# FP4 rounding in layer 2: two or three of its last steps on GpSimd, the others on VectorE

## The chip, the cores and the metric

The kernel runs on one core of a Trainium2 chip. A core has TensorE (PE, matrix products and transposes, results in PSUM), VectorE (DVE), ScalarE (ACT), GpSimd (POOL[...]) and SyncE (SP, a queue for DMAs). Each engine works through its own queue in order, and the queues wait for one another by semaphores. The metric is the device time of one execution in microseconds (us); lower is better. The median of three runs before the change is 2027.1 us (2026.68 to 2034.26).

## The reference

Four layers act on x of shape (4, 512, 256) in float32, that is 2048 rows. Each layer adds a cross-attention to a short context and then a feed-forward network. Layers 0, 1 and 3 have routed experts in the feed-forward; layer 2 has a plain one whose inputs and weights are rounded to FP4 in blocks of 16. Only this part is touched:

```python
def fp4_quant_dequant(x):
    xb = x.reshape(shape[:-1] + (shape[-1] // BLOCK, BLOCK))       # BLOCK = 16
    scale = jnp.max(jnp.abs(xb), axis=-1, keepdims=True) / 6.0
    scale = jnp.maximum(scale, jnp.float32(1e-12))
    xn = xb / scale
    idx = jnp.searchsorted(_MID, jnp.abs(xn))
    q = _GRID[idx] * jnp.sign(xn) * scale      # grid 0, 0.5, 1, 1.5, 2, 3, 4, 6
    return q.reshape(shape)

def fp4_linear(x, w):
    return jnp.einsum('bsk,nk->bsn', fp4_quant_dequant(x), fp4_quant_dequant(w))

def _L2_ffn_ref(x, w_gate, w_up, w_down):      # 256 -> 704 -> 256
    gate = fp4_linear(x, w_gate)
    y = fp4_linear(x, w_up)
    h = jax.nn.silu(gate) * y
    return fp4_linear(h, w_down)

x = x + _L2_xattn_ref(_layernorm(x, axis=-1), ctx_1024)
x = x + _L2_ffn_ref(_layernorm(x, axis=-1), L2_ffn_w_gate, L2_ffn_w_up, L2_ffn_w_down)
```

Layer 2's attention picks, for each row, the context row with the largest cosine and adds it ("alignment" below).

## The kernel before

The 2048 rows are held in SBUF as 16 tiles x[t] of 128 rows and 256 columns; four tiles make a group (one batch entry). The kernel runs the layers one after another. Layer 2 is the function `l2`, from about 1375 to 1600 us of the profiled execution.

The rounding is `fp4` (from L1437). `fp4_scale` first makes the block maxima (L1430), the scales (L1433) and their reciprocals (L1434). Then, on VectorE: multiply by the reciprocal into f_y (L1450), mask out the exponent into f_c (L1455), bound it from below and multiply by a constant so that f_c is the number to add (L1456), add f_c (L1457) and subtract it again (L1458), which rounds to the FP4 grid. The last step, multiplying by the scale into the output (L1459), goes to the engine in the argument `last`, and all three callers pass GpSimd. The callers are:

- `l2_weights`, for 18 pieces of the weights, run during layer 0 (278 to 563 us);
- `quantized(t)` in `l2`, for the 256 normalized columns of tile t, giving xq. TensorE transposes xq (L1538, into ps_xq) and ScalarE copies the result to SBUF (xqT, L1540);
- `gated` in `l2`, for the 704 gated columns, giving hq. TensorE transposes hq (L1512, ps_hT), ScalarE copies (hqT, L1513).

The loop over 16 tiles runs `up` (16 matrix-product records into four PSUM banks, ps_f, L1549), then `quantized` of the next tile, then `gated` (ScalarE's SiLU L1559 and VectorE's product h, L1560, two halves), then `down` of the tile before (ps_fd, L1571, and the addition to x, L1572). Among the tiles of one group, the alignment of the next group (`l2_xattn`: L317 to L325, L357, L1405, L691 to L703, L1413 to L1422) and its second normalization (`normed`) are woven in. The buffers f_y, f_c, xq and hq have two copies of each width.

No order is written by hand in this stage: `in_order` covers the routed experts' blocks and some other parts, not `l2`. The framework's planner puts the instructions in each engine's queue, so the order seen in the trace isn't the order of the text; it starts instructions of layer 3 (on GpSimd, the additions of a bias to x, L608) from 1549 us on. On GpSimd the last additions of layer 1's expert results (L1033) end at about 1403 us.

Of the kernel before, what the change touches and what calls it, by code (L numbers as in the profile page):

```python
# [17 lines left out]
ALU = mybir.AluOpType  # L18
# [1017 lines left out]
class Layers(Net):  # L1036
# [397 lines left out]
        nc.vector.reciprocal(rs, sc)  # L1434
        return sc, rs

    def fp4(self, tmp, out, src, last, scale=None):  # L1437


        nc = self.nc  # L1440
        rows, n = src.shape
        G = n // 16

        def blocks(t):
            return t.rearrange("p (g k) -> p g k", k=16)

        sc, rs = scale or self.fp4_scale(src)
        y, c = (tmp(t, n)[:rows] for t in ("f_y", "f_c"))

        nc.vector.scalar_tensor_tensor(  # L1450
            blocks(y), blocks(src), 1.0 - 2.0**-23, rs[:, :, None].to_broadcast([rows, G, 16]), ALU.mult, ALU.mult
        )


        nc.vector.tensor_scalar(c.bitcast(I32), y.bitcast(I32), 0x7F800000, None, ALU.bitwise_and)  # L1455
        nc.vector.tensor_scalar(c, c, 1.0, 1.5 * 2.0**22, ALU.max, ALU.mult)  # L1456
        nc.vector.tensor_tensor(y, y, c, ALU.add)  # L1457
        nc.vector.tensor_tensor(y, y, c, ALU.subtract)  # L1458
        last.tensor_tensor(blocks(out), blocks(y), sc[:, :, None].to_broadcast([rows, G, 16]), ALU.mult)  # L1459

    def l2_weights(self, pool):

        nc, d = self.nc, self.d
        F = 704
        pieces = [(n, at, t * P, 0) for n, at in (("w_gate", W2_GATE), ("w_up", W2_UP)) for t in range(6)]
        pieces += [("w_down", W2_DOWN, t * P, c) for t in range(NC) for c in range(0, F, E)]
        ws = []

        def load():
            name, _, r0, c0 = pieces[len(ws)]  # L1470
            w = pool.tile([P, E], F32, tag="w2in", name="w2in", bufs=3)
            w = w[: min(P, d[name].shape[0] - r0), : min(E, d[name].shape[1] - c0)]
            nc.scalar.dma_start(w, d[name][r0 : r0 + w.shape[0], c0 : c0 + w.shape[1]])
            ws.append(w)

        load()
        load()
        yield
        def turned(k, wq):
            name, at, r0, c0 = pieces[k]  # L1480
            rows, cols = wq.shape
            ps = self.tr.tile([P, NC, P], F32, tag="tr", name="ps_wq")
            wT = pool.tile([P, NC, P], F32, tag="w2T", name="wqT")
            for k, r in enumerate(min(P, cols - f) for f in range(0, cols, P)):
                nc.tensor.transpose(ps[:r, k, :rows], wq[:, k * P : k * P + r], self.ident[:rows, :rows])
                nc.scalar.copy(wT[:r, k, :rows], ps[:r, k, :rows])
                to = at + (c0 // P + k) * E + r0 if name == "w_down" else at + k * F + r0
                nc.scalar.dma_start(self.w2q[:r, to : to + rows], wT[:r, k, :rows])

        wq = None  # L1490
        for k in range(len(pieces)):
            if k:
                turned(k - 1, wq)
            if len(ws) < len(pieces):
                load()
            w = ws[k]
            rows, cols = w.shape
            scale = self.fp4_scale(w)
            yield
            room = pool.tile([P, 3, E], F32, tag="w2y", name="w2y")  # L1500
            y, c, wq = (room[:rows, k, :cols] for k in range(3))
            self.fp4(lambda tag, n: {"f_y": y, "f_c": c}[tag], wq, w, nc.gpsimd, scale)
            yield
        turned(k, wq)

# [9 lines left out]
    def l2(self, moe):  # L1515
        nc = self.nc
        F, H = 704, 352
        with self.room("l2") as pool:
            wq = pool.tile([P, W2_END], F32, tag="w2", name="w2", bufs=1)
            whole = W2_END - E  # L1520
            nc.sync.dma_start(wq[:, :whole], self.w2q[:, :whole])
            nc.sync.dma_start(wq[: F - 5 * P, whole:], self.w2q[: F - 5 * P, whole:])
            wg, wu = (wq[:, a : a + NC * F].rearrange("p (c f) -> p c f", c=NC) for a in (W2_GATE, W2_UP))
            wd = wq[:, W2_DOWN:].rearrange("p (f e) -> p f e", e=E)
            cnT = self.l2_context(pool)
            xns = {}

            def tmp(tag, n):
                return pool.tile([P, n], F32, tag=f"{tag}{n}", name=tag)

            def quantized(t):

                g, i = divmod(t, GT)
                xq = pool.tile([P, E], F32, tag="xq", name="xq")
                self.fp4(tmp, xq, xns[g][:, i], nc.gpsimd)
                ps = self.tr.tile([P, NC, P], F32, tag="tr", name="ps_xq")
                for c in range(NC):
                    nc.tensor.transpose(ps[:, c], xq[:, c * P : (c + 1) * P], self.ident)  # L1538
                xT = pool.tile([P, NC, P], F32, tag="xqT", name="xqT")
                nc.scalar.copy(xT, ps)  # L1540
                return xT

            def up(xT):
                pss = []
                for k in range(2):
                    for w in (wg, wu):
                        ps = self.mm.tile([P, 512], F32, tag="mm", name="ps_f")
                        for c in range(NC):
                            nc.tensor.matmul(  # L1549
                                ps[:, :H], xT[:, c], w[:, c, k * H : (k + 1) * H], start=(c == 0), stop=(c == NC - 1)  # L1550
                            )
                        pss.append(ps)
                return pss

            def gated(pss):
                h = pool.tile([P, F], F32, tag="h", name="h")
                for k in range(2):
                    s = pool.tile([P, H], F32, tag="fs", name="fs")
                    nc.scalar.activation(s, pss[2 * k][:, :H], AF.Silu)  # L1559
                    nc.vector.tensor_tensor(h[:, k * H : (k + 1) * H], s, pss[2 * k + 1][:, :H], ALU.mult)  # L1560
                hq = pool.tile([P, F], F32, tag="hq", name="hq")
                self.fp4(tmp, hq, h, nc.gpsimd)
                return hq

            def down(t, hq):
                hT = pool.tile([P, 6, P], F32, tag="hqT", name="hqT")
                self.rows_to_columns(hq, lambda f0, n, r: hT[:r, f0 : f0 + n])
                po = self.acc.tile([P, 512], F32, tag="acc", name="ps_fd")
                for f in range(6):
                    r = min(P, F - f * P)  # L1570
                    nc.tensor.matmul(po[:, :E], hT[:r, f], wd[:r, f], start=(f == 0), stop=(f == 5))  # L1571
                nc.vector.tensor_tensor(self.x[t], po[:, :E], self.x[t], ALU.add)  # L1572

            def normed(g):
                xns[g] = pool.tile([P, GT, E], F32, tag="l2xn", name="l2xn")
                self.layernorm(g, xns[g])

            for t in range(NT):  # L1580
                moe.load(pool, t, nc.scalar if t // GT == 1 else nc.sync)
            for t in range(2 * GT):
                moe.take(t, nc.vector if t < GT else nc.gpsimd)
            self.l2_xattn(pool, 0, cnT)
            normed(0)
            xT, last = quantized(0), None
            for t in range(NT):
                g, i = divmod(t, GT)
                if g + 1 < B:
                    if i == 0:  # L1590
                        if g + 2 < B:
                            for k in range(GT):
                                moe.take((g + 2) * GT + k, nc.gpsimd)
                        self.l2_xattn(pool, g + 1, cnT)
                    elif i == 2:
                        normed(g + 1)
                pss = up(xT)
                if t + 1 < NT:
                    xT = quantized(t + 1)
                hq = gated(pss)  # L1600
                if t:
                    down(t - 1, last)
                last = hq
            down(NT - 1, last)
# [77 lines left out]
```

## Time and profile before

| What | Value |
|---|---|
| median of three runs | 2027.1 us |
| profiled execution, its own time | 2033.3 us |
| its span, first to last instruction | 2031.5 us |
| mean granted TensorE clock | 0.921 |
| L1457 and L1458 in `l2`, 128x256, undisturbed | about 0.42 us each |
| L1459 to xq, median of 16 | 0.621 us |
| L1459 to hq, median of 16 | 1.386 us |
| L1033, the same 128x256 addition: VectorE, GpSimd (median) | 0.416 us, 0.724 us |
| waits of TensorE's weight loads at L1512 for hq, 1400 to 1600 us | 8.7 us, 10 times |

A group line of the profile gives source line, engine, operation, output from inputs and shapes, the count, then the busy time in us and the mean of one in ns, then the engine's idle time before the group and what ended it. A timeline line gives the start in us, the duration in us, the engine and the instruction; brackets hold idle time before it. A windows line gives for each engine the busy us in that stretch and the number of instructions, then the granted clock. In the 40 slices each digit is the busy share in tenths.

### The profile page before, as it was taken

What the parts mean: (1) busy time and instruction counts of PE and PEld (TensorE: products, weight loads), DVE (VectorE), ACT (ScalarE), POOL (GpSimd) and SP (SyncE); (2) the same over time, 40 slices, a digit from 0 to 9 for tenths busy, and PEclk for the clock granted to TensorE, in tenths of its full rate; (3) what the DMA queues carried; (4) which work ended last, traced back from release to release, by engine and by line L of the source; (5) the groups of instructions that cost most, each with busy time, mean ns of one, the idle gap of its engine ahead of it and who ended that gap; (6) DMA issues with size and microseconds to landing.
All of it is one profiled execution on the core that took longest, in us unless ns stands there. A gap on an engine that the chain in (4) does not pass through costs nothing.

```text
span 2031.5 us, 25639 instructions
## 1 busy us (share of the span) xinstructions
PE 1716.2 (84%) x8740; PEld 975.9 (48%) x8740; DVE 974.0 (48%) x2778; ACT 668.2 (33%) x1254; POOL 420.3 (21%) x590
## 2 busy tenths in 40 slices
PE   4874999999959978899999878994998887599994
PEld 2443666666624533344443344443665443355662
DVE  3644344444445333445454435446899564333333
ACT  3341322222243341335344522223445333122221
POOL 1033011111150010222222322224113112311112
PEclk8986999999979987999999989996899898699997
DMA  9613878787420000000000018772000001598895
GB/s 290 182 43 127 343 292 285 283 292 279 157 93 1 17 23 0 1 1 17 6 3 20 19 34 283 263 270 88 1 0 1 12 4 40 181 313 296 305 316 170
DMA packets 111042, 271.85 MB, mean 134 GB/s; under 512 B 15488, under 2 KB 73024, under 8 KB 100800
## 3 DMA queue, kind: packets, MB, share of 16 engines
q1 hardware_dynamic: 81728, 227.35, 33.0%
q0 software_dynamic: 10176, 28.00, 3.6%
q10 hardware_dynamic: 19008, 14.86, 2.3%
q8 instruction: 70, 1.15, 0.2%
q14 instruction: 60, 0.49, 0.1%
HBM read 220.75 MB, written 49.42 MB: 133 GB/s over the span
## 4 chain that ended last, share of the span: by engine, by line
PE 63%; DVE 14%; ACT 5%; issue 3%; POOL 3%; DMA 2%; SPq 0%; ACTq 0%; DVEq 0%; POOLq 0%
PE ps_gu L938 20%; PE ps_de L980 9%; PE ps_ms L1127 4%; PE ps_mo L1165 3%; DVE mq L1132 2%; PE ps_he L967 2%; PE ps_p L592 2%; PE ps_mx L1142 2%; PE ps_f L1549 2%; POOL xs L827 2%; PE ps_bc L571 1%; PE ps_ms L1130 1%; PE ps_xT L357 1%; PE ps_xe L924 1%; PE ps_cy L577 1%
## 5 line engine op out<-in xcount | busy, mean ns | idle before, releaser
L938 PE MATMUL ps_gu<-e_wgu,e_xT 128*128 128x352 f32 (+1 forms) x1088 | 417.8, 524 | 4.7 <-DVE e_xT L930 0.8
L938 PEld LDWEIGHTS ps_gu<-e_wgu,e_xT 128*128 128x128 f32 x1088 | 197.2, 191 | 143.9 <-issue 74.0
L980 PE MATMUL ps_de<-e_wd,e_hT 128*128 128x256 f32 x932 | 232.3, 385 | 3.8 <-ACT e_hT L288 1.5
L955 DVE TENSOR_TENSOR e_h<-e_s,ps_gu 128x352 f32<-128x352 f32 (+2 forms) x155 | 83.5, 538 | 295.5 <-PE ps_gu L938 226.9
L983 POOL DMA_INDIRECT ys<-e_y,e_to x116 | 112.4, 969 | 522.4 <-ACT e_y L982 399.5
L980 PEld LDWEIGHTS ps_de<-e_wd,e_hT 128*128 128x128 f32 x932 | 172.1, 189 | 79.5 <-issue 42.3
L954 ACT ACTIVATE e_s<-ps_gu 128x352 f32<-128x352 f32 (+2 forms) x155 | 74.0, 477 | 327.6 <-PE ps_gu L938 323.5
L1132 DVE TENSOR_REDUCE mq<-ps_ms 128x2 f32<-128x256 f32 (+3 forms) x128 | 105.7, 825 | 137.8 <-PE ps_ms L1130 136.5
L982 ACT ACTIVATE e_y<-ps_de,e_wt 128x256 f32<-128x256 f32 x116 | 54.9, 473 | 259.4 <-PE ps_de L980 248.1
L1144 ACT ACTIVATE mpr<-ps_mx 128x1024 f32<-128x1024 f32 (+3 forms) x128 | 90.0, 703 | 138.7 <-PE ps_mx L1142 135.5
L1127 PE MATMUL ps_ms<-mkT,mqT 32*128 32x512 f32 (+3 forms) x512 | 111.1, 512 | 22.7 <-DVE mq L1132 21.6
L827 POOL DMA_INDIRECT xs<-xn,e_at x96 | 93.9, 978 | 135.3 <-DVE ln_rs L322 75.7
L1142 PE MATMUL ps_mx<-mqm,mkT 32*128 32x128 f32 (+3 forms) x512 | 105.6, 489 | 1.1 <-ACT mpr L1144 1.1
L1146 POOL TENSOR_SCALAR_AFFINE_SELECT mpr<-mpr 128x256 f32<-128x256 f32 x128 | 51.8, 407 | 238.6 <-ACT mpr L1144 238.5
L1165 PE MATMUL ps_mo<-mpr,va 128*32 128x128 f32 (+3 forms) x512 | 96.4, 457 | 3.0 <-POOL mpr L1146 3.0
L357 PE MATMUL ps_xT<-consts_sb,xn 128*128 128x128 f32 x256 | 52.4, 340 | 50.9 <-ACT xn L325 36.1
L967 PE MATMUL ps_he<-consts_sb,e_h 128*128 128x128 f32 x466 | 76.2, 278 | 11.9 <-DVE e_h L955 7.9
L1549 PE MATMUL ps_f<-w,xqT 128*128 128x352 f32 x256 | 84.7, 472 | 1.2 <-ACT xqT L1540 1.2
L924 PE MATMUL ps_xe<-consts_sb,e_x 128*128 128x128 f32 x232 | 51.4, 292 | 36.6 <-DMA e_x<-xs 33.6
L927 DVE COPY e_xT<-ps_xe 128x256 f32<-128x256 f32 x78 | 33.0, 423 | 98.4 <-PE ps_xe L924 98.4
L537 PE MATMUL ps_cx<-q,kbd 32*128 32x512 f32 x256 | 45.0, 803 | 39.5 <-ACT cpr L543 39.5
L1127 PEld LDWEIGHTS ps_ms<-mkT,mqT 32*128 32x128 f32 x512 | 40.8, 195 | 77.6 <-DVE mq L1132 54.4
(314 smaller groups left out, 2769.0 us busy)
## 6 DMA issues: line engine op xcount, KB each, us to landing
e_wgu<-in_e0gu SPq DMA_DIRECT2D x39, 1408.0 KB, 6.1
e_wgu<-in_e3gu SPq DMA_DIRECT2D x39, 1024.0 KB, 5.4
e_wd<-in_e0d SPq DMA_DIRECT2D x39, 768.0 KB, 5.6
e_wd<-in_e3d SPq DMA_DIRECT2D x39, 512.0 KB, 5.6
e_wgu<-in_e1gu SPq DMA_DIRECT2D x38, 512.0 KB, 4.0
xs<-z SPq DMA_DIRECT2D x16, 1040.0 KB, 15.4
e_x<-xs SPq DMA_DIRECT2D x116, 130.0 KB, 4.9
e_wd<-in_e1d SPq DMA_DIRECT2D x38, 256.0 KB, 4.1
```

Source lines behind the costliest of these rows:

```text
L827: r = nc.gpsimd.indirect_dma_start(out=net.xs, out_offset=bass.IndirectOffsetOnAxis(ap=at[:, k, i : i + 1], axis=0), in_=rows[:, i], in_of ...
L938: nc.tensor.matmul(ps[:, :n], xT[:, c], wgu[:, c, cols], start=(c == 0), stop=(c == NC - 1))
L955: nc.vector.tensor_tensor(h[:, k * H : (k + 1) * H], s, u, ALU.mult)
L967: self.nc.tensor.transpose(ps[:r, f - f0], h[:, f * P : f * P + r], net.ident)
L980: nc.tensor.matmul(po[:, :E], hT[:r, f], wd[:r, f], start=(f == 0), stop=(f == self.nf - 1))
L983: r = nc.gpsimd.indirect_dma_start(out=net.ys, out_offset=bass.IndirectOffsetOnAxis(ap=at, axis=0), in_=y, in_offset=None)
L1127: nc.tensor.matmul(ps[:, r, :n], st.qT[o][rows, diag], st.kT[o][rows, :n], start=True, stop=False)
L1132: nc.vector.tensor_reduce(st.q[:, i, at : at + 2, HD], ps[:, :, :n], AX.X, ALU.max, negate=True)
L1142: nc.tensor.matmul(ps[:, r, :n], st.kT[o][rows, keys], st.qm[o][rows, j * P :], start=True, stop=True)
L1144: nc.scalar.activation(pr[:, :, :n], ps[:, :, :n], AF.Exp, scale=HD**-0.5)
L1165: nc.tensor.matmul(st.po[32 * n : 32 * n + 32, j * P :], st.va[:, j, at : at + 32], pr[:, r, : S - j * P], start=(j == 0), stop=(j == GT - 1),
L1549: nc.tensor.matmul(ps[:, :H], xT[:, c], w[:, c, k * H : (k + 1) * H], start=(c == 0), stop=(c == NC - 1))
```

## The change

`fp4` gets a number, `late`, in place of the engine: so many of the last three steps (add, subtract, multiply by the scale) go to GpSimd, the others stay on VectorE. The list in the new line ends in three GpSimd engines for 3, in VectorE, GpSimd, GpSimd for 2, and in VectorE, VectorE, GpSimd for 1. The weights pass 1, the normalized rows 3, the gated rows 2. What is computed is the same.

```diff
-    def fp4(self, tmp, out, src, last, scale=None):
+    def fp4(self, tmp, out, src, late, scale=None):
...
         nc.vector.tensor_scalar(c, c, 1.0, 1.5 * 2.0**22, ALU.max, ALU.mult)
-        nc.vector.tensor_tensor(y, y, c, ALU.add)
-        nc.vector.tensor_tensor(y, y, c, ALU.subtract)
+        add, subtract, last = ([nc.vector] * 3 + [nc.gpsimd] * late)[-3:]
+        add.tensor_tensor(y, y, c, ALU.add)
+        subtract.tensor_tensor(y, y, c, ALU.subtract)
         last.tensor_tensor(blocks(out), blocks(y), sc[:, :, None].to_broadcast([rows, G, 16]), ALU.mult)
...
-            self.fp4(lambda tag, n: {"f_y": y, "f_c": c}[tag], wq, w, nc.gpsimd, scale)
+            self.fp4(lambda tag, n: {"f_y": y, "f_c": c}[tag], wq, w, 1, scale)
...
-                self.fp4(tmp, xq, xns[g][:, i], nc.gpsimd)
+                self.fp4(tmp, xq, xns[g][:, i], 3)
...
-                self.fp4(tmp, hq, h, nc.gpsimd)
+                self.fp4(tmp, hq, h, 2)
```

## The prediction

> **What bounds the kernel now.** I read the page first for where the change acts, then windows over that stretch, then its groups by form, the chain of waits and the timeline.
>
> ```profile
> span 2031.5 us, 25639 instructions
> PE 1716.2 (84%) x8740; PEld 975.9 (48%) x8740; DVE 974.0 (48%) x2778; ACT 668.2 (33%) x1254; POOL 420.3 (21%) x590
> ...
> PE   4874999999959978899999878994998887599994
> ...
> DVE  3644344444445333445454435446899564333333
> ```
>
> Over the whole span VectorE is busy only 48%, but each slice is 50.8 us, and slices 29 to 31 (1422 to 1574 us) show 8, 9, 9: this is layer 2's feed-forward, the only place where the edited arguments change anything. Windows there:
>
> ```profile
> core 0: us, PE busy (x) PEld busy (x) DVE busy (x) ACT busy (x) POOL busy (x), PEclk, DMA share, GB/s
> 1400.00:1600.00 200.00, 175.06 (x712) 116.52 (x711) 173.15 (x448) 94.64 (x203) 48.05 (x53) 0.93 0.00 1
> ...
> 1485.00:1495.00 10.00, 10.00 (x41) 6.50 (x40) 10.00 (x25) 8.19 (x21) 2.11 (x3) 1.00 0.00 0
> 1545.00:1555.00 10.00, 8.65 (x37) 5.64 (x36) 10.00 (x22) 4.38 (x10) 5.77 (x6) 1.00 0.00 0
> 1555.00:1565.00 10.00, 7.78 (x34) 5.04 (x33) 9.90 (x22) 4.98 (x10) 5.83 (x6) 1.00 0.00 1
> 1565.00:1575.00 10.00, 9.92 (x41) 6.61 (x40) 7.21 (x16) 4.15 (x9) 1.38 (x1) 1.00 0.01 2
> ```
>
> TensorE and VectorE are both nearly full: two limits that take turns. At 1545 to 1565 VectorE is full and TensorE is not; at 1565 it is the other way round. Adding the 10 us windows from 1405 on, TensorE stands idle for 21 us, 5 of them in the first window (filling); so 16 us is all that can be won by removing waits. The chain of waits agrees: of the 179 us in its longest pieces between 1400 and 1600, 91 us lie on TensorE, 77 (0.43) on VectorE, 7 on GpSimd. GpSimd enters six times: as hq at 1429.50, 1494.90, 1565.47, 1575.85, as xq at 1409.16 and 1536.10.
>
> ```profile
> L1457 DVE TENSOR_TENSOR f_y<-f_y,f_c 128x704 f32<-128x704 f32 x16 | 14.1, 881 | 0.1
> L1458 DVE TENSOR_TENSOR f_y<-f_y,f_c 128x704 f32<-128x704 f32 x16 | 14.1, 880 | 0.0
> L1457 DVE TENSOR_TENSOR f_y<-f_y,f_c 128x256 f32<-128x256 f32 x16 | 10.2, 640 | 0.0
> L1458 DVE TENSOR_TENSOR f_y<-f_y,f_c 128x256 f32<-128x256 f32 x16 | 7.3, 456 | 0.0
> L1459 POOL TENSOR_TENSOR hq<-f_y,f_sc 128x704 f32<-128x704 f32 x16 | 22.4, 1400 | 100.5 <-DVE f_y L1458 66.4 <-PE ps_f L1549 11.8 <-PE ps_xq L1538 9.0
> L1459 POOL TENSOR_TENSOR xq<-f_y,f_sc 128x256 f32<-128x256 f32 x16 | 11.6, 726 | 46.2 <-DVE f_y L1458 25.4 <-PE ps_xq L1538 7.5 <-DVE ln_sh L323 5.6
> ```
>
> Rows two to five are the moved operations, except L1457 at 704 columns, which stays. The 256-column add averages 640 ns, though the same form is 420 when nothing disturbs it. The timeline shows why:
>
> ```profile
> 1545.14 0.16 DVE L1433 TENSOR_SCALAR f_sc<-f_am 128x16 f32<-128x16 f32 x1
> 1545.16 1.39 POOL L1459 TENSOR_TENSOR hq<-f_y,f_sc 128x704 f32<-128x704 f32 x1 [2.76 <-DVE f_y L1458]
> 1545.22 0.16 DVE L322 RECIPROCAL ln_rs<-ln_sd 128x4 f32<-128x4 f32 x1
> 1545.31 1.52 DVE L1457 TENSOR_TENSOR f_y<-f_y,f_c 128x256 f32<-128x256 f32 x1
> 1546.60 0.76 PE L1512 MATMUL ps_hT<-consts_sb,hq 128*128 128x128 f32 x5 [1.34 <-POOL hq L1459]
> 1546.75 0.51 DVE L1560 TENSOR_TENSOR h<-fs,ps_f 128x352 f32<-128x352 f32 x1
> ```
>
> The add starts at 1545.31 but ends at 1546.83, 0.28 us after GpSimd's operation ends: it stood still until then, and h, behind it in VectorE's queue, came late.
>
> **What the Trainium skill says.** "SBUF — State Buffer", section "Who interferes with whom": a VectorE instruction with two SBUF inputs, or in a two-port mode, and a GpSimd instruction that reads SBUF exclude one another; whoever starts first keeps the port pair for the whole instruction. The trace agrees, with 1.52 us in place of 0.42, and for the smallest operation too: a 128x16 L1433 at 1495.14 takes 1.27 us beside hq. "Perfetto Trace Analysis", section "Optimizing Scalar/DVE Operations", warns that offloading between these two may therefore not help. "GPSIMD Engine Reference", section "4.1 Engine selection", gives about twice the time for two-input operations; here the same 128x256 addition (L1033, both engines) takes 416 ns on VectorE and 724 on GpSimd, 1.74 times.
>
> **The change part by part.**
>
> The weights' call keeps two steps on VectorE and one on GpSimd: no cost.
>
> Removed from VectorE. Instructions overlap at their ends, so I count start to start: 0.34 us at 256 columns, 0.80 at 704. Per tile 0.34 + 0.34 + 0.80 = 1.48, times 16 = 23.7 us. With the moved adds go their own blocked times: (640 - 420) x 16 = 3.5 and (456 - 420) x 16 = 0.6. Together 27.8 us.
>
> Added to GpSimd. Add and subtract at 256: 0.72 each from L1033, 1.44 x 16 = 23.0. The subtract at 704 is not in the trace; L1459 at 704, whose second input is a repeated scale, takes 1.39 (lower bound), L1033 stretched in proportion gives 0.72 x 704/256 = 1.98 (upper). I take 1.6, x 16 = 25.6. Sum 48.6 us; GpSimd goes from 48 to 97 busy in the 200, so it doesn't become the bound by load.
>
> What it blocks. In 1400 to 1600 VectorE's blocked time, mean less undisturbed mean times count, is 12.4 us: L1457 3.5, L1458 0.6, L1455 1.5, L1433 1.5, L323 1.6, L1450 1.7, L1456 1.1, L1400 0.9. Over 48 us of GpSimd this is 0.26 us per us. The added 48.6 then block 12.6 us. Unknown: the share may be 0 or, if VectorE always meets a port operation next, near 1. At 0.57 (27.8/48.6) VectorE wins nothing. I take 0.26, and VectorE is relieved by 27.8 - 12.6 = 15.2 us, 0.95 per tile. It counts where VectorE is on the path: 0.43 x 15.2 = 6.5 us.
>
> Longer latency. Row to xq: 1.44 in place of 0.68, +0.76. Gated row to hq: 1.6 in place of 0.80, +0.8. On the chain that is four hq and two xq: 3.2 + 1.5 = 4.7 us. Elsewhere the xq lateness is hidden: xq is one or two tiles ahead (done at 1542.39, transposed at 1544.87, cover 2.5 us). Where hq's lateness is hidden, TensorE's matmuls of the next tile (L1549) do it; there is little: TensorE's weight loads wait for hq ten times already.
>
> Waits and queues. The adds now queue on GpSimd behind layer 3's bias additions (L608, 12 times, 10.3 us, from 1549 on); behind a waiting add stands the other row's hq. f_c comes free after GpSimd's subtract, up to about 2 us later; two buffers of each width mean that only the row after next needs it, some 10 us on: nothing, save at the start, where three rows run close together and a 128x16 scale already waits 0.36 us for xq.
>
> Sum against the profiled execution (2033.3 us, span 2031.5): -6.5 + 4.7 = -1.8, so 2031.5. The median of the runs is 2027.1, 6 us below that execution; the same difference gives 2025.
>
> A check by hand with the order kept, port held by whoever asks first. Tile from 1527.06: the subtract runs 1532.57 to 1534.17, two scales and a reciprocal slip between, VectorE reaches the operation of 1537.16 about 0.7 us early; TensorE waits for xqT there until 1536.88 anyway. Tile from 1537.16: add, subtract and scale of xq alternate with L1450, L1455 and L1456, hq's subtract runs 1544.49 to 1546.09, hq ends at 1547.68 (1546.55 before), and the scale behind it holds h back from 1546.75 to 1547.85: 1.1 late. One better, one worse: no clear sign.
>
> **The rivals.** About 0.5% (10 us) is what a measurement of this kernel can tell from no change.
>
> First, VectorE was the real limit, and TensorE closes up: the whole 15.2 counts less one longer first row and last gated row (0.76 + 0.8), -13.6: about 2013. For it: three 10 us windows with VectorE at 9.9 or more and TensorE at 8.7 or less. Against: only 16 us of TensorE idleness exist, part of it behind ScalarE's table loads and layer 2's alignment chain.
>
> Second, slower by one mechanism: GpSimd's back-to-back operations hold the port, a small VectorE operation stands behind them, h and hq come late, and TensorE waits at hq's transposes (L1512). Price: 1.1 us as in the second replay, at the ten tiles where it waits for hq already, 11, and 0.76 + 0.8 at start and end: +12.6, 2040. It decides when the blocked share passes 0.57.
>
> Third, no order is written by hand in this stage, so the planner may arrange the longer GpSimd steps otherwise; this may tip the sum either way by what the replays differ, within the two above.
>
> **How the numbers follow.** No measurable change around 2025: 0.40 (own range 2017 to 2037); faster near 2013: 0.36; slower near 2040: 0.24. With share 0 the sum would be 0.43 x 27.8 - 4.7 = 7 us won; with share 1, 0.43 x 20.8 + 4.7 = 14 lost. The range for 8 in 10 reaches past these to the two rivals: 2007 to 2042.
>
> **What would show it.** Right: VectorE's busy time in this stage falls by some 10 to 16 us while L1433, L1455 and L1450 lengthen; GpSimd's doubles; a GpSimd 256-column addition takes 0.72, the 704-column subtract 1.4 to 2.0; waits of L1512 for hq grow. Wrong: blocked time far off 0.26 per us, an operation of GpSimd outside its bounds, the chain of waits moving wholly to TensorE (first rival) or to GpSimd's f_y and hq (second), or a change outside 1400 to 1600.

## The result and the profile after

The changed kernel is slower: a median of 2045.13 us (2037.37 to 2053.4, 11 runs) against 2033.42 us of the kernel before on the same chip (2026.68 to 2048.35, 11 runs), a ratio of 1.0049 with a 95% interval of 1.003 to 1.0069, that is 6 to 14 us. A second set on another occasion gave 1.0048 (1.0033 to 1.0062). The forecast of 2025 started from 2027.1, the median of three runs; with eleven runs the kernel before stands at 2033.42, so 6.3 of the 20 us between 2025 and 2045.13 were there before the change. The granted TensorE clock does not explain the rest: in the second set it averaged 0.9157, against 0.9145 for the kernel before. The profiled execution took 2040.63 us (span 2038.9), 7.3 more than that of the kernel before. In the changed kernel the line numbers from L1458 on are one higher: L1458 adds, L1459 subtracts, L1460 multiplies, L1513 transposes hq, L1561 makes h.

The loss lies in layer 2. These lines give the first and last start of two operations, L1422 (an alignment is added to x) and the addition of `down` to x, before and after:

```profile
L1422 DVE TENSOR_TENSOR x<-ps_al,x x16: 414/415/425, 1399.4 to 1516.3; 128x256 f32<-128x256 f32 x16
L1572 DVE TENSOR_TENSOR x<-ps_fd,x x16: 410/421/426, 1436.5 to 1598.9; 128x256 f32<-128x256 f32 x16
...
L1422 DVE TENSOR_TENSOR x<-ps_al,x x16: 412/415/426, 1395.3 to 1514.5; 128x256 f32<-128x256 f32 x16
L1573 DVE TENSOR_TENSOR x<-ps_fd,x x16: 411/420/425, 1433.5 to 1602.5; 128x256 f32<-128x256 f32 x16
```

From the first of these to the last the stage takes 199.5 us before and 207.2 after (210.0 in the changed kernel's second profile). The code ahead of it is the same, yet its end moves between 1395 and 1410 us from one execution to the next, so a fixed window of time does not always hold the same work.

The windows view of the changed kernel, with the same stretch of 200 us first and then the 10 us about tile 10; below it the page's line for the whole program:

```profile
core 0: us, PE busy (x) PEld busy (x) DVE busy (x) ACT busy (x) POOL busy (x), PEclk, DMA share, GB/s
1400.00:1600.00 200.00, 166.11 (x693) 112.08 (x694) 159.47 (x384) 92.95 (x199) 93.30 (x91) 0.93 0.00 1
1540.00:1550.00 10.00, 1.96 (x8) 1.04 (x6) 9.83 (x15) 1.69 (x5) 9.86 (x11) 0.78 0.00 0
...
PE 1713.1 (84%) x8740; PEld 977.0 (48%) x8740; DVE 964.2 (47%) x2730; ACT 668.7 (33%) x1254; POOL 471.6 (23%) x638
```

In the 200 us VectorE's busy time fell by 13.7 us (173.15 to 159.47) and GpSimd's rose by 45.3 (48.05 to 93.30). But TensorE's fell too, by 9 us: it does the same work, so less of the work lies in these 200 us. Over the whole program, where nothing else was changed, VectorE's busy time fell by only 9.8 us (974.0 to 964.2; to 965.4 in the second profile) and GpSimd's rose by 51.3 (420.3 to 471.6). In 1540 to 1550 TensorE does almost nothing, while VectorE and GpSimd are full.

The groups by form in the same stretch, of the steps that moved and of their neighbours on VectorE:

```profile
L1459 POOL TENSOR_TENSOR f_y<-f_y,f_c 128x704 f32<-128x704 f32 x16 | 26.9, 1678 | 70.6 <-DVE f_y L1458 68.4 <-DVE l_m L1400 2.2
L1460 POOL TENSOR_TENSOR hq<-f_y,f_sc 128x704 f32<-128x704 f32 x16 | 22.8, 1427 | 1.0
L1459 POOL TENSOR_TENSOR f_y<-f_y,f_c 128x256 f32<-128x256 f32 x16 | 13.0, 811 | 1.0
L1458 POOL TENSOR_TENSOR f_y<-f_y,f_c 128x256 f32<-128x256 f32 x16 | 12.4, 774 | 8.8 <-DVE f_c L1456 8.6 <-DVE f_sc L1433 0.2
L1450 DVE SCALAR_TENSOR_TENSOR f_y<-l2xn,f_rs 128x256 f32<-128x256 f32 x16 | 10.6, 661 | 0.1
...
L1455 DVE TENSOR_SCALAR f_c<-f_y 128x256 int32<-128x256 int32 x16 | 8.7, 546 | 0.1
```

The added GpSimd time is 26.9 + 13.0 + 12.4 = 52.3 us. The steps of the normalized rows that stayed on VectorE took over the blocking of the steps that left: L1450 at 256 columns now averages 661 ns (477 before), L1455 546 (275 before).

The waits view, TensorE's weight loads, first before and then after; the three numbers are the sum in us, the count and the longest:

```profile
PEld ps_hT L1512 <- POOL hq L1459: 8.7, 10, 2.2
...
PEld ps_sim L1405 <- DVE xnT L290: 1.1, 1, 1.1
...
PEld ps_hT L1513 <- POOL hq L1460: 22.2, 10, 10.3
...
PEld ps_sim L1405 <- DVE xnT L290: 6.8, 3, 4.5
```

The timeline of seven of the ten waits for hq, brackets holding the wait; the last two lines are tiles 10 and 11 of the kernel before:

```profile
1428.62 0.53 PEld L1513 LDWEIGHTS ps_hT<-consts_sb,hq 128*128 128x128 f32 x5 [2.19 <-POOL hq L1460]
...
1436.17 0.53 PEld L1513 LDWEIGHTS ps_hT<-consts_sb,hq 128*128 128x128 f32 x5 [1.34 <-POOL hq L1460]
...
1487.30 0.53 PEld L1513 LDWEIGHTS ps_hT<-consts_sb,hq 128*128 128x128 f32 x5 [1.42 <-POOL hq L1460]
...
1498.39 0.53 PEld L1513 LDWEIGHTS ps_hT<-consts_sb,hq 128*128 128x128 f32 x5 [2.35 <-POOL hq L1460]
...
1532.98 0.42 PEld L1513 LDWEIGHTS ps_hT<-consts_sb,hq 128*128 128x128 f32 x4 [1.42 <-POOL hq L1460]
...
1551.98 0.93 PEld L1513 LDWEIGHTS ps_hT<-consts_sb,hq 128*128 128x128 f32 x5 [10.25 <-POOL hq L1460]
...
1597.91 0.53 PEld L1513 LDWEIGHTS ps_hT<-consts_sb,hq 128*128 128x128 f32 x5 [2.54 <-POOL hq L1460]
...
1546.60 0.53 PEld L1512 LDWEIGHTS ps_hT<-consts_sb,hq 128*128 128x128 f32 x5 [1.58 <-POOL hq L1459]
...
1557.54 0.42 PEld L1512 LDWEIGHTS ps_hT<-consts_sb,hq 128*128 128x128 f32 x4 [2.20 <-POOL hq L1459]
```

Tiles 0, 1, 5, 6, 9 and 15 wait 0.8 to 2.0 us longer than before (the first four shown: 2.19, 1.34, 1.42 and 2.35 in place of 1.07, 0.56, 0.17 and 1.19). Tile 10 waits 10.25 us where it was 1.58; tile 11, the longest before with 2.20, waits no more. GpSimd's timeline ahead of tile 10's hq:

```profile
1537.69 0.72 POOL L1458 TENSOR_TENSOR f_y<-f_y,f_c 128x256 f32<-128x256 f32 x1
1538.49 0.72 POOL L1459 TENSOR_TENSOR f_y<-f_y,f_c 128x256 f32<-128x256 f32 x1
1539.18 7.65 POOL L608 TENSOR_TENSOR x<-x,rows_sb 128x256 f32<-128x256 f32 x8
1546.78 0.72 POOL L1458 TENSOR_TENSOR f_y<-f_y,f_c 128x256 f32<-128x256 f32 x1
1547.59 2.35 POOL L1459 TENSOR_TENSOR f_y<-f_y,f_c 128x256 f32<-128x256 f32 x2
1550.01 1.91 POOL L1460 TENSOR_TENSOR hq<-f_y,f_sc 128x704 f32<-128x704 f32 x1
```

GpSimd works through its queue in order. Eight of layer 3's additions (L608) and a normalized row's add stand ahead of the gated row's subtract (one of the two in the line with x2) and so of hq. In the kernel before, the planner had put those additions behind this hq: there L608 begins at 1549.39, and hq of tile 10 ends at 1546.55. VectorE's timeline shows a second effect, here the first and the last of the row's own steps ahead of the subtract:

```profile
1539.42 1.41 DVE L1450 SCALAR_TENSOR_TENSOR f_y<-h,f_rs 128x704 f32<-128x704 f32 x1
...
1544.15 1.41 DVE L1458 TENSOR_TENSOR f_y<-f_y,f_c 128x704 f32<-128x704 f32 x1
```

The row's add ends only at 1545.56, so the row itself stands in GpSimd's queue for about 2.7 us, not for all of the 7.65. But beside those additions VectorE's steps are drawn out: this stretch takes 6.1 us, and 3.5 before (1540.27 to 1543.78). From the end of h to the end of hq tile 10 takes 15.1 us in place of 8.4: 1.9 more on VectorE although it has one step less, 2.7 in the queue, 1.7 for the subtract and 0.5 more for the multiply. TensorE's wait grew by 8.7 us, 2.0 more than that, because TensorE came to these transposes 2.0 us sooner after h. A longer wait for hq is therefore not all lost time.

The times at which h is complete show where the stage loses. From tile 0 to tile 9 it takes 106.7 us before and 106.3 after; from 9 to 12 it takes 31.2 and 39.3 (38.7 in the second profile); from 12 to 15, 27.8 and 26.9. Up to tile 9 nothing is lost; the loss is where tile 10 stalls. Two things were to be told apart: the queue at this one place, and the GpSimd time as such.

### The profile page after: what moved, and what is told of

It reads as the page before. It is cut to its first block, busy times and chain, and to the rows that moved or that the text cites. A ratio compares the mean times of both kernels' runs of the same rounds, so it can differ in the third digit from the quotient of the medians.

```text
span 2038.9 us, 25635 instructions
## 1 busy us (share of the span) xinstructions
PE 1713.1 (84%) x8740; PEld 977.0 (48%) x8740; DVE 964.2 (47%) x2730; ACT 668.7 (33%) x1254; POOL 471.6 (23%) x638
## 4 chain that ended last, share of the span: by engine, by line
PE 62%; DVE 13%; ACT 6%; issue 4%; POOL 4%; DMA 2%; SPq 0%; ACTq 0%; DVEq 0%; POOLq 0%
PE ps_gu L938 20%; PE ps_de L980 9%; PE ps_ms L1127 4%; PE ps_mo L1165 3%; DVE mq L1132 2%; PE ps_he L967 2%; PE ps_p L592 2%; PE ps_mx L1142 2%; POOL xs L827 2%; PE ps_f L1550 1%; PE ps_bc L571 1%; PE ps_ms L1130 1%; PE ps_xT L357 1%; PE ps_xe L924 1%; PE ps_cy L577 1%
## 5 line engine op out<-in xcount | busy, mean ns | idle before, releaser
L357 PE MATMUL ps_xT<-consts_sb,xn 128*128 128x128 f32 x256 | 53.0, 346 | 48.6 <-ACT xn L325 33.9
```

## The experiments

All were timed against the kernel before on the same chip. "Held additions" means that layer 3's sixteen L608 additions are placed behind the last gated row's multiply in GpSimd's queue, with the other queues' order unchanged:

```diff
-            self.nc.gpsimd.tensor_tensor(x, x, self.row(bias), ALU.add)
+            with self.tc.issue_after(self.l2_end) if self.l2_end else nullcontext():
+                self.nc.gpsimd.tensor_tensor(x, x, self.row(bias), ALU.add)
```

The table has the ratio with its interval, the busy time of VectorE and GpSimd in the whole program (all other work in it is the same), and TensorE's waits for hq and xnT from the stage's first transposes of xq to its last addition of `down` (us, from one profile each).

| Run | Ratio (95%) | VectorE | GpSimd | hq | xnT |
|---|---|---|---|---|---|
| before | 1 | 974.0 | 420.3 | 8.7 | 1.1 |
| after | 1.0049 (1.003 to 1.0069) | 964.2 | 471.6 | 22.2 | 6.8 |
| e12, after again | 1.0048 (1.0033 to 1.0062) | 965.4 | 471.5 | 22.0 | 6.8 |
| e1, after, held additions | 1.0048 (1.0026 to 1.007) | 961.7 | 470.2 | 17.3 | 6.8 |
| e2, before, held additions | 1.0003 (0.9994 to 1.0011) | 973.1 | 418.8 | 6.9 | 1.1 |
| e3, e2 and eight planted adds | 1.0017 (1.0008 to 1.0027) | 974.6 | 424.8 | 9.8 | 1.1 |
| e4, e2 and the moved steps twice | 1.0103 (1.0081 to 1.0125) | 991.8 | 471.8 | 12.6 | 3.2 |
| e5, e2 and memsets | 1.0006 (0.9989 to 1.0024) | 977.2 | 442.9 | 8.1 | 1.9 |
| e6, normalized rows only | 0.9993 (0.9983 to 1.0004) | 968.3 | 446.3 | 9.4 | 4.2 |
| e7, gated rows only | 1.0003 (0.9991 to 1.0016) | 969.0 | 444.6 | 13.2 | 3.0 |
| e8, e1 with GpSimd in text order | 1.0204 (1.0179 to 1.023) | 954.8 | 468.2 | 2.6 | 1.9 |
| e9, e1 with rows held back | 1.0034 (1.0016 to 1.0052) | 962.1 | 471.2 | 19.0 | 2.9 |
| e10, e9, additions free | 1.0044 (1.0027 to 1.0061) | 964.4 | 474.3 | 22.6 | 3.0 |
| e11, e7 with rows held back | 0.9993 (0.9979 to 1.0007) | 966.5 | 446.3 | 12.8 | 1.3 |
| e13, e1, subtract of tile 10 back | 1.0029 (1.0017 to 1.0041) | 962.7 | 468.7 | 16.2 | 6.8 |
| e14, e1, last group's rows back | 1.0029 (1.0012 to 1.0046) | 965.6 | 463.4 | 14.9 | 6.8 |
| e15, e1, five subtracts back | 1.0007 (0.9996 to 1.0018) | 962.3 | 467.1 | 15.6 | 2.2 |
| e16, one step, normalized rows | 0.9992 (0.9979 to 1.0005) | 967.6 | 433.5 | 7.2 | 2.1 |
| e17, nine gated rows only | 0.9999 (0.9985 to 1.0014) | 968.6 | 432.7 | 9.2 | none |
| e18, e17 and normalized rows | 1.0015 (1.0001 to 1.0029) | 960.8 | 462.4 | 14.2 | 2.2 |

**The queue at tile 10 (e1, e2, e3).** e1 is the changed kernel with held additions, e2 the control.

> The changed kernel, with layer 3's sixteen bias additions (L608) placed behind the last gated row's multiply in GpSimd's queue; every other queue is as in the changed kernel. Queue theory (the loss is the eight additions that stand ahead of one gated row's subtract at 1539 to 1547 us, with TensorE idle for 10 us): the stall goes and the ratio to the kernel before falls from 1.005 to 0.996 to 1.001; the wait of 10 us at the transposes of hq is gone. Port theory (GpSimd's longer steps block VectorE and delay hq in every tile): nothing much changes, ratio 1.003 to 1.006.

> The kernel before with the same placement of the bias additions, as the control for the run above; all other queues as before. Both theories: 0.997 to 1.001, since the additions of before stand behind gated rows that aren't late; a little gain where they kept the port from VectorE at 1549 to 1563 us.

e3 is e2 with eight 128x256 additions, whose result nothing reads, placed on GpSimd ahead of tile 10's gated row:

```diff
+                if t == 10:
+                    with self.tc.issue_after(self.hq_last.ins):
+                        for k in range(8):
+                            z = pool.tile([P, E], F32, tag="extra", name="extra", bufs=1)
+                            add = nc.gpsimd.tensor_tensor(z, xq, self.row(R_BO3), ALU.add)
```

> The kernel before with the bias additions placed late as in the control, and eight additions of 128x256 into a tile that nobody reads put into GpSimd's queue ahead of the gated row of tile 10; VectorE keeps both rounding steps. Queue theory: the 8 us stall appears without the change, ratio 1.003 to 1.006. Port theory: 6 us of port time at a price of 0.26 block some 1.5 us of VectorE, ratio 0.999 to 1.002.

e1 stayed at 1.0048, in the range of the port theory, so the queue theory in this form fell. In its profile the stall shrinks but does not go away with the additions. GpSimd's timeline of e1 (L1460 adds, L1461 subtracts, L1462 multiplies there):

```profile
1549.83 1.30 POOL L1460 TENSOR_TENSOR f_y<-f_y,f_c 128x256 f32<-128x256 f32 x1 [2.77 <-DVE f_c L1458]
1551.21 2.35 POOL L1461 TENSOR_TENSOR f_y<-f_y,f_c 128x256 f32<-128x256 f32 x2
1553.65 1.39 POOL L1462 TENSOR_TENSOR hq<-f_y,f_sc 128x704 f32<-128x704 f32 x1
```

A normalized row's add stands at the head of GpSimd's queue and waits 2.77 us for f_c from VectorE; the gated row's subtract is behind it. VectorE's timeline of e1 shows what that costs the gated row:

```profile
1547.26 0.88 DVE L1452 SCALAR_TENSOR_TENSOR f_y<-h,f_rs 128x704 f32<-128x704 f32 x1
...
1549.67 0.88 DVE L1460 TENSOR_TENSOR f_y<-f_y,f_c 128x704 f32<-128x704 f32 x1
```

Its own add ends at 1550.55, after the wait of 2.77 is over, so it stands in the queue for about 1.35 us, and its steps on VectorE are no longer drawn out (3.3 us in place of 6.1). TensorE's wait shrank from 10.25 to 5.5 us, not to 1.6. By the traces that is some 5 us saved; the timed runs do not confirm it (e1 against after, and e9 against e10, differ by less than their intervals), so what the additions' place costs stays open between nothing and about 4 us. From tile 9 to tile 12 e1 still takes 34.6 us, and e2 29.8.

e3 missed the queue theory's range and lies in that of the port theory: the planted additions made a wait of 4.4 us, not the stall of 8. Against e2 TensorE's waits for hq grew by 2.9 us, all of it at tile 10, and the time by 0.0014 of 2035 us, 2.8 us (intervals overlap a little). At this one place a microsecond of waiting for hq seems to cost about a microsecond; e7 below shows that this is no rule for the stage.

**GpSimd time without relief (e4, e5).** e4 is e2 with the moved steps computed once more on GpSimd, into a tile that nothing reads, behind each multiply; nothing is taken off VectorE:

```diff
+        for _ in range(extra):
+            self.fp4_last = nc.gpsimd.tensor_tensor(tmp("f_z", n), y, c, ALU.subtract)
```

> The kernel before with the bias additions placed late, and the moved steps computed once more on GpSimd into a tile that nobody reads (two of 128x256 per normalized row, one of 128x704 per gated row, each behind the multiply): the change's port time without its relief of VectorE and without its place on the path. Port theory: 49 us more of port time with no relief, ratio 1.004 to 1.010. Queue theory (the port costs about 0.26 us per us, of which half counts): 12.6 us blocked, ratio 1.002 to 1.004.

The groups of e4:

```profile
L1463 POOL TENSOR_TENSOR f_z<-f_y,f_c 128x704 f32<-128x704 f32 x16 | 28.0, 1753 | 0.0
L1463 POOL TENSOR_TENSOR f_z<-f_y,f_c 128x256 f32<-128x256 f32 x32 | 25.7, 824 | 0.0
```

GpSimd has 53.7 us more, about what the change adds. It costs 0.0100 of 2035 us, 20 us: 0.38 us for each, just above the range of the port theory and far above that of the queue theory. The profiled stage is 15 us longer than e2's, and the granted clock averaged 0.914 against 0.918, so part of the 20 may lie outside the stage. That much GpSimd time, with VectorE not relieved, is dear; the change pays part of it back.

e5 has memsets in that place, three for a normalized row and one for a gated row, which only write, into a tile that nothing reads (the line that keeps each behind its multiply is left out):

```diff
-            self.fp4_last = nc.gpsimd.tensor_tensor(tmp("f_z", n), y, c, ALU.subtract)
+                self.fp4_last = nc.gpsimd.memset(tmp("f_z", n), 0.0)
```

> The kernel before, with additional GpSimd work that writes only: three memsets of 128x256 behind each normalized row's multiply and one of 128x704 behind each gated row's, into a tile that nothing reads. The queues of TensorE, VectorE and ScalarE are the same as in the kernel before, layer 3's additions stand at the end. Estimate from L625 and L1286 of the kernel before: 48 x 0.31 + 16 x 0.69 = 26 us of GpSimd. Port theory (what hurts is GpSimd's reading of SBUF): a memset reads nothing, ratio 0.998 to 1.002. Occupancy theory (what hurts is only that GpSimd's queue is longer busy and xq and hq come later): the doubled steps cost 0.39 us for each us of GpSimd, so 10 us here, ratio 1.003 to 1.006.

```profile
L1464 POOL MEMSET f_z<- 128x256 f32 x48 | 15.3, 358 | 0.0
...
L1464 POOL MEMSET f_z<- 128x704 f32 x16 | 11.0, 686 | 0.0
```

26.3 us of GpSimd and no measurable cost: the number that the port theory named. Its reason was wrong in part, since VectorE was blocked all the same. Summing over VectorE's operations of 1395 to 1630 us what each took beyond the lower quartile of its form in all traces gives about 15 us for e2, 26 for e5 and 34 for e4. So 10 us of blocking cost nothing that shows, and hq's waits hardly grew (8.1 us in e5, 6.9 in e2). That does not show what makes e4 dear: e5 adds half the GpSimd time of e4, and a run with as much write-only time is missing.

**One part alone (e6, e7).**

```diff
-                self.fp4(tmp, hq, h, 2)
+                self.fp4(tmp, hq, h, 1)
```

e6 is this with held additions; e7 leaves the gated rows at 2 and gives the normalized rows 1.

> Only the normalized rows' add and subtract moved (3), the gated rows as before (1); layer 3's additions at the end of the stage. Port theory: each part costs by its GpSimd time, 23 to 25 us here of about 50 in all, so about half of the loss: 1.001 to 1.004. Path theory (what hurts is the longer way from h to hq, which TensorE waits for): xq is made one or two tiles ahead, so VectorE's relief counts and nothing is lost: 0.996 to 1.001.

> Only the gated rows' subtract moved (2), the normalized rows as before (1); layer 3's additions at the end of the stage. Port theory: 26 to 28 us of GpSimd, about half of the loss: 1.001 to 1.004. Path theory: the whole loss or more is here: 1.004 to 1.007.

Neither theory was right for both: 0.9993 and 1.0003. The parts do not add up: alone nothing, together 10 us. The waits view of e7 shows the balance:

```profile
PEld ps_hT L1515 <- POOL hq L1462: 13.2, 9, 3.6
```

TensorE waits 6.3 us longer for hq than in e2 and yet the time is the same (the interval leaves 3 us either way), while VectorE's busy time fell by only 4.1 us (973.1 to 969.0). So either relief is worth more than the forecast gave it, or part of the longer wait is no loss, since TensorE comes sooner; these runs do not tell which. With both parts hq's waits are 17.3 to 22.2 us, and the time is longer.

**The order of rows (e8 to e12).** e8 forces GpSimd's queue in this stage into the order of the text, with held additions:

```diff
-        with banks():
+        with banks(), self.in_order(POOL):
             self.l2(moe)
```

> The changed kernel with GpSimd's queue in this stage in the order of the text, so that the steps of one normalized row stand between those of two gated rows, never two rows or more ahead of a gated row's; layer 3's additions at the end. Port theory: the same GpSimd reading, the loss stays: 1.003 to 1.007. Queue theory in its second form (a gated row's subtract stands behind several normalized rows' steps, as 2.8 us of waiting and two rows in the profile of the run with late additions): most of the loss goes, 0.998 to 1.002.

It took 1.0204 (1.0179 to 1.023). GpSimd's timeline of e8 shows the reason:

```profile
1423.32 0.62 POOL L1462 TENSOR_TENSOR xq<-f_y,f_sc 128x256 f32<-128x256 f32 x1
1440.12 1.67 POOL L1461 TENSOR_TENSOR f_y<-f_y,f_c 128x704 f32<-128x704 f32 x1 [16.18 <-DVE f_y L1460]
```

GpSimd idles 16.18 us for a gated row, and all later normalized rows are behind it: TensorE's waits moved from hq to xq (42.3 us in 1415 to 1645, of which 10 at the start stand in the changed kernel too). Neither theory's range holds it. The planner's order had been the better one; this form of the queue theory was not tested by it.

The planner had also reordered VectorE. In the changed kernel the first steps of the normalized rows 4 to 7 stand ahead of the second half of gated row 2 and of row 3, rows 13 and 14 ahead of row 10, and in e7 likewise except for row 14; in the kernel before they stand behind. e9 holds nine normalized rows where e6 has them:

```diff
+            ROWS = {4: (2, 1), 5: (3, 0), 6: (3, 0), 7: (3, 1), 10: (6, 0), 11: (6, 1)}
+            ROWS |= {13: (10, 0), 14: (10, 0), 15: (10, 1)}
...
+                with self.tc.issue_after(hs[ROWS[t]]) if t in ROWS else nullcontext():
+                    self.fp4(tmp, xq, xns[g][:, i], 3)
```

> The changed kernel, layer 3's additions at the end of the stage, and nine normalized rows on VectorE held behind the gated products that they follow in the run with only the normalized rows moved (rows 4, 5, 6, 7 behind gated rows 2 and 3, rows 10, 11 behind 6, rows 13 to 15 behind 10). The planner of the changed kernel had put rows 4 to 7 ahead of the second half of row 2 and of row 3, and rows 13 and 14 ahead of row 10. Order theory (the steps that the planner put ahead of h, drawn out by GpSimd, make h late, and each part alone loses nothing because its GpSimd time or its order is milder): most of the loss goes, 0.996 to 1.001. Port theory (the GpSimd time itself costs): the loss stays, 1.003 to 1.006.

> As the run before with the same order of rows, but layer 3's additions where the planner puts them. Order theory: 0.996 to 1.002, and if the additions' place costs what the two traces differ by (5 us), 0.0025 above the run before. Port theory: 1.003 to 1.007.

> Only the gated rows' subtract moved, with the same order of rows held and layer 3's additions at the end. Alone and without the order it gave 1.0003. Order theory: better than that, 0.996 to 0.9995. Port theory: 0.999 to 1.002.

> The changed kernel once more, beside the other three on the same chip: 1.003 to 1.007 by both theories, since nothing is changed; it shows how far two profiles of one kernel differ in this stage.

e10 is e9 with the additions where the planner puts them, e11 has the same rows held and only the gated rows' subtract moved. 1.0034 and 1.0044 against 1.0048 with the planner's order: outside what the order theory named, inside the port theory's ranges. The order accounts for 0.0014 of the 0.0048 by the middle values, and by the intervals for none of it with certainty. xnT's waits did fall, from 6.8 to 2.9, hq's did not (17.3 to 19.0). e11 (0.9993) lies within both theories.

**Taking single steps back (e13 to e16).** Each starts from e1.

```diff
-                self.fp4(tmp, hq, h, 2)
+                self.fp4(tmp, hq, h, 2 if t != 10 else 1)
```

is e13; e14 passes `3 if g < 3 else 1` for the normalized rows; e15 is e13 with tiles 0 to 3 as well; e16 passes 2 and 1.

> The changed kernel with layer 3's additions at the end, and the subtract of one gated row, tile 10, back on VectorE. TensorE's and ScalarE's queues are unchanged, VectorE's by that one instruction. Stall theory (a waiting normalized row's add holds the gated row's subtract in GpSimd's queue at tile 10; 5.3 us of TensorE's time in the trace with late additions): 1.0015 to 1.0035. Spread theory (the loss is about 1 us at each of ten tiles): 1.004 to 1.0055.

> As before, but the four normalized rows of the last group keep their add and subtract on VectorE (1), the gated rows all keep 2. TensorE's queue is unchanged. Stall theory: 1.001 to 1.0035. Spread theory: 1.0035 to 1.0055.

> As before, but the subtracts of five gated rows, tiles 0 to 3 and 10, back on VectorE, those tiles beside which normalized rows are rounded or TensorE starts. Stall theory, with the group start: 0.999 to 1.002. Spread theory: eleven of sixteen gated rows keep the longer way, 1.002 to 1.004.

> Only one step moved: the normalized rows' subtract (2), the gated rows as before (1), layer 3's additions at the end. It adds 12 us of GpSimd and takes 5.4 off VectorE. Both theories, near no change: 0.997 to 1.001; a gain under 0.998 would show that a smaller move pays.

All four fell in the ranges of the stall theory: 1.0029, 1.0029, 1.0007, 0.9992. One instruction of tile 10 gives back 0.0019 (e1, after and e12 together give 1.0048, plus or minus 0.001, so the gain is barely outside the intervals; against e1 alone it is within them), the four tiles at the start another 0.0022. But e13's trace shows neither the stall gone nor the gain: GpSimd's add still waits there, TensorE's wait at tile 10 is 4.3 us in place of 5.5, and the stage from L1424 to the last L1575 is as long as e1's (205.9 us both).

```profile
1551.89 1.31 POOL L1460 TENSOR_TENSOR f_y<-f_y,f_c 128x256 f32<-128x256 f32 x1 [2.77 <-DVE f_c L1458]
1553.27 1.25 POOL L1461 TENSOR_TENSOR f_y<-f_y,f_c 128x256 f32<-128x256 f32 x1
1554.49 1.38 POOL L1462 TENSOR_TENSOR hq<-f_y,f_sc 128x704 f32<-128x704 f32 x1
```

The same waiting add of 2.77 us now stands ahead of hq's multiply. So the timed gain fits the theory's numbers, and its mechanism is not shown.

**Only where the two kinds of rows do not meet (e17, e18).** The gated subtract is moved at nine tiles alone; e17 gives the normalized rows 1, e18 gives them 3, both with held additions:

```diff
-                self.fp4(tmp, hq, h, 2)
+                self.fp4(tmp, hq, h, 2 if t in (4, 7, 8, 9, 11, 12, 13, 14, 15) else 1)
```

> Only gated rows' subtracts moved, at the nine tiles 4, 7 to 9 and 11 to 15, where no normalized row's rounding lies beside them on VectorE; normalized rows as before (1), layer 3's additions at the end. If the loss comes from the meeting of the two kinds of rows: 0.996 to 1.000. If each longer way from h to hq costs TensorE something: 1.000 to 1.002.

> As the run before, with the normalized rows' add and subtract moved too (3). Meeting theory: 0.995 to 1.000, better than the normalized rows alone (0.9993). Otherwise 1.000 to 1.003, since this is the run with five gated rows taken back (1.0007) with two more taken back.

e17 costs and gains nothing (0.9999). e18 gave 1.0015, above what the meeting theory named, in the range of the other one and no better than e15. So keeping the two kinds of rows apart is not shown to be what helps, nor a way to a gain. No version beat the kernel before by more than its interval; the best, e16 and e6, stand at 0.9992 and 0.9993.

## Why the prediction was wrong

**On one footing.** The forecast was 1.8 us faster than the kernel before, from its own sum; measured is 6 to 14 us slower. The range of 2007 to 2042 was laid around the lower baseline of three runs.

**Right: the blocking.** 12.6 us were forecast. The operations that stayed on VectorE take 12.6 us more in sum over the whole trace (13.6 in the second profile). The Trainium skill, "SBUF — State Buffer", section "Who interferes with whom", describes this exclusion for an operation with two SBUF inputs, and the trace agrees again (L1450 at 256 columns, 477 to 661 ns).

**Right: GpSimd's times.** The 704-column subtract takes 1.678 us (1.6 taken, bounds 1.39 to 1.98), the 256-column steps 0.72 when undisturbed, 0.77 and 0.81 in the mean; 52.3 us in place of 48.6.

**Too large: VectorE's relief.** 15.2 us were forecast; over the whole program VectorE's busy time fell by 9.8 (8.6 in the second profile). The step "Removed from VectorE" took 0.08 us for each of the 48 removed steps, 3.8 in all, as overlap with the next; the overlap of neighbouring instructions fell by 8.6 us, since the steps that stayed follow one another less closely.

**Not settled: what relief is worth.** The forecast gave it 0.43. e7 moves the 704-column subtract alone and cannot be held against the price of the whole.

**Wrong: the longer way to hq.** This is the step that failed. "Longer latency" set 3.2 + 1.5 = 4.7 us, and "Waits and queues" named what stands ahead on GpSimd, layer 3's additions and a waiting add ahead of hq, but put no price on it. Measured, TensorE's waits for hq, forecast to cost 3.2, grew by 13.5 us (8.7 to 22.2; to 22.0 in the second profile), of which 8.7 at tile 10 (1.58 to 10.25). The other tiles come to 4.8, near the forecast in part by luck: six tiles add 7.5 us, and tiles 11 to 13 give 3.1 back. Its waits for xq hardly changed (9.6 to 10.0 at the start, 0.7 to none later) in place of the 1.5. The second hand replay walks tile 10 itself and found 1.1 us; it had no additions of layer 3 beside that row, neither in the queue nor holding the port.

With the measured terms the sum is -0.43 x 9.8 + 13.5 = +9.3 us, against 7.3 between the two profiled executions and 6 to 14 by the ratio. This is a fit after the fact. Longer waits for xnT (1.1 to 6.8 us) would come on top, and TensorE's sooner arrival would come off.

**Wrong: a buffer put at nothing.** VectorE's 128x16 scale now waits for GpSimd's multiply into xq 3.8 us in four waits, against 0.6 in the kernel before; the prediction had seen this wait at the start and given it no price. What it costs the total is not shown.

**Wrong: order held.** Both hand replays assumed the order of the kernel before. The planner arranged the queues anew, and the third rival, "within the two above", had no price of its own; e9 puts the VectorE part of it at 0 to 0.3% or so.

**The second rival** came nearest, in place (TensorE waiting at hq's transposes), sign and size: 12.6 us against 10. The size is in part luck, since its form was off: not 1.1 us at each of ten tiles, but 4.8 us spread over the tiles and 8.7 in one stall. Its threshold did not decide: the blocked share, 12.6/52.3 = 0.24, stayed far below 0.57. Hq's lateness does not need VectorE to lose time in all.

**Still open:** why the two parts lose so much more together. In the profiles e6 and e7 also lose from tile 9 to tile 12 (30.8 and 32.0 us, e2 29.8, e1 34.6) and win it back on the way from tile 0 to tile 9 (103.9 and 105.1, e2 106.8, e1 105.9). Waits for hq alone do not order the runs. Waits for hq and xnT together nearly do, among the runs that move steps: up to 16.2 us (e6, e7, e11, e16, e17) no loss shows, 16.4 and 17.8 (e18, e15) go with 0.0015 and 0.0007, 21.7 to 25.6 (e14, e9, e13, e1, e10) with 0.0029 to 0.0048, and 28.8 and 29.0 (e12, after) with 0.0048 and 0.0049. That was found afterwards and tested by no run, and e4 (15.8 us, 1.0103), where VectorE is slowed and not relieved, does not fit.

## What to carry to other kernels

Moving steps off a nearly full engine relieved it here by less than the durations said, and an in-order engine got a queue: a result that it used to finish with one step now stands behind other rows' steps. Price the worst tile, not only the mean: list what stands ahead of the moved step and what runs beside the row's other steps, other layers' work included, and what each waits for. Compare profiles between events of the program, not in a fixed window of time. Try the parts alone before the whole: here each was harmless and the sum was not.

## What the runs showed of the hardware

A write-only GpSimd operation held VectorE's small single-input steps as well. The timeline of e5:

```profile
1545.62 1.38 POOL L1461 TENSOR_TENSOR hq<-f_y,f_sc 128x704 f32<-128x704 f32 x1 [2.25 <-DVE f_y L1460]
1545.66 1.99 DVE L1435 TENSOR_SCALAR f_sc<-f_am 128x16 f32<-128x16 f32 x1
...
1546.94 0.69 POOL L1464 MEMSET f_z<- 128x704 f32 x1
```

The 128x16 scale, 0.16 us undisturbed, ends at 1547.65, 0.02 us after the memset and 0.65 after the multiply: it stood still through both. Over all sixteen such scales the mean went from 258 ns in e2 to 540 in e5. The same section of the Trainium skill says that VectorE in a two-port mode is excluded by GpSimd, and that one with two SBUF inputs is not by a write-only one; the first agrees with this line if the scale runs in such a mode, which no run here shows by itself.
